# Placing the graph steps of the next groups inside the LSTM of the last layer

## The chip, the cores and the metric

The kernel runs on one core of a Trainium2 chip. The metric is the device time of one execution in microseconds (us), here the median of several runs. Five engines work side by side, each through its own queue of instructions: TensorE (PE), VectorE (DVE), ScalarE (ACT), GpSimd (POOL), and SyncE (SP), which in this kernel issues the DMAs.

## The reference

The program is four graph layers on `x` of shape 128 x 64 x 256 (128 graphs of 64 nodes with 256 features), each added to its input and normalised. Only the last layer matters here. It makes two graph convolutions and then, for each step length p = 1, 2, 3, 4 in turn, runs an LSTM over windows of p nodes and writes the last hidden state over the last node of each window; the next p reads what the one before wrote.

```python
h = jax.nn.relu(jnp.einsum('ts,bsh->bth', adj, x @ Wg0 + bg0))
h = jax.nn.relu(jnp.einsum('ts,bsh->bth', adj, h @ Wg1 + bg1))
for p in range(1, MAX_SKIP + 1):
    nw = Tv // p
    wins = h[:, :nw * p, :].reshape(Bv * nw, p, Hd)
    last = _lstm_last(Wih[p - 1], Whh[p - 1], bih[p - 1], bhh[p - 1], wins)
    idx = jnp.arange(nw) * p + (p - 1)
    h = h.at[:, idx, :].set(last.reshape(Bv, nw, Hd))
...
x = _layernorm(x + _L3_gnn_ref(x, adj, ...), axis=-1)
```

All data are fp32.

## The kernel before, in words

The last layer works on 8 groups of 16 graphs, `g` = 0 to 7. For each group there are three kinds of work.

**The convolutions**, `gcn(g, half, bank, name)`, once for each half of a group. It is a generator of 8 steps, n = 0 to 7. Steps 0 and 1 are the blocks: each loads 256 KB of the layer's residual (`x2r`, L875), applies the batch normalisation of layer 2 with two ACT instructions (L879, in place on the resident tile `A`), turns the data through DRAM (`turned`: a DVE transpose L848, one DMA to the scratch tensor `way` L851, four DMAs back L853), adds on DVE (L884), layer-normalises (DVE statistics, POOL L83 and L97) and stores two pieces to DRAM (L895). Group 0 alone turns by PE (L889) in place of the DMAs. Step 2 multiplies by the neighbour matrix (PE L866, copies L902 on DVE and L903 on ACT), steps 3 and 4 by the first weight (PE L909, DVE L911, ACT L913), steps 5 and 6 by the second (PE L921, DVE L924), step 7 by the neighbours again (PE L866, DVE L932 and ACT L933), which fills the group's tile `H`.

**The LSTM**, `lstm(g)`, is a generator of 22 units, u = 0 to 21. A unit is one of the two 128-row halves `j` of the hidden state, for one time step: units 0 to 3 are p = 1 (two stretches of windows), 4 to 7 p = 2, 8 to 13 p = 3, 14 to 21 p = 4. In a unit PE adds the input part of the gates (L970) and, from the second time step on, the hidden part (L976) in PSUM banks `l` (5 of them), ACT takes the gates out (L982), DVE and POOL form the cell (L985 to L989), ACT takes its tanh (L990). With the second unit of a time step DVE writes the hidden state: `hid` (L999) for the next time step, or back into `H` (L999) at the end of p = 1, 2, 3, or `hd` (L997) at the end of p = 4. So every odd unit ends with a hand-over that a later matmul waits for.

**The output**, `final(g, s)`, for four residues s of the node: a copy on POOL (L1011), the same `turned`, an add (L1024), a layer normalisation and two stores (L1033). It is traced behind units 14, 16 and 18 of its own group, and behind unit 0 of the next group for s = 3.

The order on each engine is not written by hand. A planner takes the instructions as they are traced, gives the earlier traced the higher priority, and on each engine issues what it expects to be ready at that moment. An instruction that is traced late can therefore stand early in an engine's queue, if its inputs are expected early. While group g is in the LSTM, the steps of group g + 1 are traced between its units: `steps_of` gives their order (both halves' blocks, then the rest of half 0, then the rest of half 1), and the loop at the end hands out 16 steps evenly over the first 19 units. All buffers involved rotate: `st` has 5 (two for `turned`, one for an output or a step's result), `g` 3 PSUM banks, `x2r` 4, `way` 4, `hT` 2.

Of the kernel before, what the change touches and what calls it, by code (L numbers as in the profile page):

```python
# [34 lines left out]
SKIP = 4  # L35
# [6 lines left out]
def kernel(ctx: ExitStack, tc: tile.TileContext, i, out):  # L42
    nc = tc.nc
# [41 lines left out]
    def layernorm(dst, src, n, engine):  # L85

        st = small.tile([P, n, 6], F32, name="ln_st", bufs=6)
        mv = small.tile([P, n, 2], F32, name="ln_mv", bufs=6)
        both = small.tile([P, 2, n], F32, name="ln_rs", bufs=6)
        rs, ng = both[:, 0, :], both[:, 1, :]  # L90
        for r in range(n):
            nc.vector.bn_stats(st[:, r, :], src[:, r, :])
            nc.vector.bn_aggr(mv[:, r, :], st[:, r, :])
        rsqrt(rs, mv[:, :, 1], n)
        nc.vector.tensor_scalar_mul(ng, mv[:, :, 0], -1.0)  # L95
        for r in range(n):
            engine.tensor_scalar(dst[:, r, :], src[:, r, :], ng[:, r:r + 1], rs[:, r:r + 1],  # L97
                                 op0=OP.add, op1=OP.mult)
# [725 lines left out]
    NG = NB // GB  # L824
    assert GB * N == 2 * QT

    def gbank(shape):
        return ps.tile([P] + shape, F32, name="g", bufs=3)
# [15 lines left out]
    def turned(src):  # L844


        t = work.tile([P, 4, 4, 32], F32, name="st", bufs=ST)
        nc.vector.transpose(t, src.rearrange("p n (j t) -> p j n t", t=32))  # L848
        o = work.tile([P, 4, 4, 32], F32, name="st", bufs=ST)
        way = dram.tile([P, 4, P], F32, name="way", bufs=4)  # L850
        nc.sync.dma_start(way, t.rearrange("p j n f -> p j (n f)"))  # L851
        for j in range(4):
            nc.sync.dma_start(o[j * 32:(j + 1) * 32].rearrange("t i n f -> t i (n f)"),  # L853
                              way[:, j, :].rearrange("(i t) x -> t i x", t=32))
        return o.rearrange("p i (c m) f -> p c m i f", m=KD)
# [80 lines left out]
    GCN_STEPS = 8  # L936
# [67 lines left out]
    def final(g, s, pieces=1):  # L1004

        if s == SKIP - 1:
            h = lasts.pop(g)
        else:
            h = work.tile([P, 2, KD, P], F32, name="hd", bufs=3)
            for c in range(2):  # L1010
                nc.gpsimd.tensor_copy(h[:, c].rearrange("p k (w b) -> p k w b", b=GB),  # L1011
                                      Hs[g].rearrange("p k (c w s) b -> p c k w s b", c=2, s=SKIP)[:, c, :, :, s, :])

        rows = [v[g * GB:(g + 1) * GB].rearrange("b (c w s) d -> s c w b d", c=2, s=SKIP)[s]
                for v in (x3_dram, out_view)]
        xr = work.tile([P, 2, D], F32, name="x3r")
        for c in range(2):
            nc.sync.dma_start(xr[:, c, :], rows[0][c])
        o = work.tile([P, 2, D], F32, name="st", bufs=ST)
        for cs in ([(0, 1)] if pieces == 1 else [(0,), (1,)]):  # L1020
            r = slice(cs[0], cs[-1] + 1)
            if pieces == 1:
                xv = xr.rearrange("p c (m i f) -> p c m i f", m=KD, f=32)
                nc.vector.tensor_add(xv, turned(h.rearrange("p c m t -> p (c m) t")), xv)  # L1024
            else:
                ht = gbank([2, D])
                for c in cs:
                    for k in range(KD):
                        nc.tensor.transpose(ht[:, c, k * P:(k + 1) * P], h[:, c, k], ident)
                nc.vector.tensor_add(xr[:, r], ht[:, r], xr[:, r])  # L1030
            layernorm(o[:, r], xr[:, r], len(cs), nc.gpsimd)
            for c in cs:
                nc.sync.dma_start(rows[1][c], o[:, c, :])  # L1033

    def steps_of(g):

        if g:
            parts = [gcn(g, half, gbank, "hT") for half in range(2)]
            order = [0, 0, 1, 1] + [0] * (GCN_STEPS - 2) + [1] * (GCN_STEPS - 2)
        else:  # L1040
            parts = [gcn(g, 0, gbank, "hT"), gcn(g, 1, lbank, "hid")]
            order = [0, 0, 1, 1] + [0, 1] * (GCN_STEPS - 2)
        for half in order:
            next(parts[half])
            yield

    for _ in steps_of(0):
        pass
    n_units = sum(-(-(N // p) // (QT // GB)) * p * KD for p in range(1, SKIP + 1))
    first4 = n_units - SKIP * KD  # L1050
    for g in range(NG):

        side = steps_of(g + 1) if g + 1 < NG else iter(())
        n_side, done = 2 * GCN_STEPS, 0
        for u, _ in enumerate(lstm(g)):
            if u == 0 and g:
                final(g - 1, SKIP - 1)
            s, odd = divmod(u - first4, 2)
            if not odd and 0 <= s < SKIP - 1:
                final(g, s)  # L1060
            while done < min(n_side, (u + 1) * n_side / (n_units - 2)):
                next(side, None)
                done += 1
    final(NG - 1, SKIP - 1, pieces=2)


# [38 lines left out]
```

## Time and profile before

| what | value |
|---|---|
| runs | 2173.53, 2174.7, 2179.28 us; median 2174.7 |
| profiled execution | 2175.27 us, its span 2173.4 us |
| the LSTM's part of the span | about 832 to 2173 us: seven groups of some 168.6 us, and the last one of some 161 |
| LSTM matmuls on PE, whole kernel | L970 789.2 us, L976 436.2 us |
| a unit of p = 4 with both parts, on PE | 3.45 us for 16 records of L970, 3.45 us for 16 of L976 |
| granted TensorE clock, mean | 0.986 |
| DMA share of 16 engines, queue 1 | 17.7% |

A time such as "789.2" is busy time: what the records of that line last in sum. "Idle before ... <-" in a row says for how long the engine stood still before that instruction and what ended it. PE's records count every 128-row fp32 multiplication twice.

### The profile page before, as it was taken

To read this page: it belongs to the slowest core of one execution; us is meant where nothing else is said; L and a number is where in the kernel's file an instruction comes from. 1 tells how busy PE (TensorE), PEld (TensorE's weight loads), DVE (VectorE), ACT (ScalarE), POOL (GpSimd) and SP (SyncE) were. 2 spreads that over 40 slices of the span, in tenths; PEclk is the share of its full clock that TensorE was granted. 3 is DMA by queue.
4 is the path that set the end of the run, shared out by engine and by line. 5 is a ranking of instruction groups with operands and counts; after the bars stand their busy time and mean duration, and the time that the engine had idled before them with its cause. 6 is when DMAs were issued, how large, how long until landed. Compare 5 with 4: busy or idle time off the path is not lost.

```text
span 2173.4 us, 29437 instructions
## 1 busy us (share of the span) xinstructions
PE 2083.1 (96%) x11463; PEld 1340.8 (62%) x11463; DVE 863.1 (40%) x2054; ACT 946.2 (44%) x1825; POOL 414.7 (19%) x569
## 2 busy tenths in 40 slices
PE   6999999998999979999999999999999999999997
PEld 4667677775454444576576577477468468468466
DVE  7355555454543444134233323323323423423223
ACT  3766666765338153234233334333333333333332
POOL 1123332433210012011111111111211211202012
PEclk9999999999999979999999999999999999999999
DMA  4023213232222022012112101201201201201001
GB/s 124 20 42 52 50 44 50 52 52 42 42 86 59 0 87 79 0 44 67 46 31 66 60 29 54 73 14 55 88 10 58 89 4 60 73 1 59 20 5 54
DMA packets 169275, 105.54 MB, mean 49 GB/s; under 512 B 86832, under 2 KB 152368, under 8 KB 168880
## 3 DMA queue, kind: packets, MB, share of 16 engines
q1 hardware_dynamic: 167280, 101.70, 17.7%
q8 instruction: 90, 1.47, 0.3%
q0 software_dynamic: 1024, 1.05, 0.2%
q10 hardware_dynamic: 832, 0.92, 0.1%
q14 instruction: 49, 0.40, 0.1%
HBM read 59.59 MB, written 44.04 MB: 48 GB/s over the span
## 4 chain that ended last, share of the span: by engine, by line
PE 80%; ACT 6%; DVE 6%; DMA 3%; issue 2%; POOL 1%; SPq 1%; DVEq 0%; POOLq 0%; ACTq 0%
PE l L970 31%; PE l L976 19%; PE pz L707 5%; PE pz L772 4%; PE e L311 3%; PE g L909 2%; PE g L921 2%; PE m L283 2%; PE m L218 2%; PE m L286 2%; PE g L866 1%; DMA way<-st 1%; PE z L320 1%; PE m L401 1%; PE m L197 1%
## 5 line engine op out<-in xcount | busy, mean ns | idle before, releaser
L970 PE MATMUL l<-H,wih 128*128 128x256 f32 (+2 forms) x2496 | 789.2, 471 | 9.4 <-ACT gate_g L990 3.9
L970 PEld LDWEIGHTS l<-H,wih 128*128 128x128 f32 x2496 | 469.9, 190 | 302.3 <-issue 189.2
L976 PE MATMUL l<-hid,whh 128*128 128x256 f32 (+2 forms) x1536 | 436.2, 437 | 2.1 <-DVE hid L999 2.1
L976 PEld LDWEIGHTS l<-hid,whh 128*128 128x128 f32 x1536 | 291.8, 190 | 130.9 <-issue 61.2
L982 ACT ACTIVATE gate_i<-l,bias 128x256 f32<-128x256 f32 (+2 forms) x176 | 100.1, 569 | 517.8 <-PE l L976 445.9
L985 DVE TENSOR_TENSOR gate_i<-gate_i,gate_g 128x256 f32<-128x256 f32 (+2 forms) x96 | 48.5, 506 | 432.7 <-ACT gate_g L982 432.6
L986 POOL TENSOR_TENSOR cell<-gate_f,cell 128x256 f32<-128x256 f32 (+2 forms) x96 | 84.4, 880 | 670.6 <-ACT gate_f L982 663.4
L83 POOL TENSOR_TENSOR ln_rs<-ln_rs,mhalf 128x2 f32<-128x2 f32 (+2 forms) x97 | 79.1, 815 | 689.5 <-DVE ln_rs L95 689.1
L322 ACT ACTIVATE u<-z 128x1024 f32<-128x1024 f32 x128 | 130.4, 1026 | 57.4 <-PE z L320 56.6
L982 ACT ACTIVATE gate_g<-l,bias 128x256 f32<-128x256 f32 (+2 forms) x176 | 100.3, 570 | 98.3 <-PE l L970 50.1
L990 ACT ACTIVATE gate_g<-cell 128x256 f32<-128x256 f32 (+2 forms) x176 | 90.0, 511 | 88.7 <-DVE cell L989 45.7
L982 ACT ACTIVATE gate_o<-l,bias 128x256 f32<-128x256 f32 (+2 forms) x176 | 99.4, 565 | 61.9 <-PE l L976 54.0
L707 PE MATMUL pz<-A,w 128*128 128x512 f32 x256 | 113.1, 595 | 0.0
L989 DVE TENSOR_TENSOR cell<-gate_i,gate_g 128x512 f32<-128x512 f32 (+2 forms) x80 | 50.0, 624 | 138.1 <-ACT gate_g L982 137.9
L294 DVE TENSOR_TENSOR qs<-m,qs 64x256 fp32r<-64x256 f32 x128 | 54.0, 422 | 124.4 <-ACT qs L293 122.7
L320 PE MATMUL z<-gath_r,qs 128*128 128x512 f32 x256 | 99.4, 476 | 0.6 <-ACT u L322 0.4
L707 PEld LDWEIGHTS pz<-A,w 128*128 128x128 f32 x256 | 47.9, 190 | 55.3 <-issue 53.6
L283 PE MATMUL m<-wq,tT 128*128 128x260 f32 x256 | 72.4, 406 | 8.1 <-ACT yT L391 5.4
L982 ACT ACTIVATE gate_f<-l,bias 128x256 f32<-128x256 f32 (+2 forms) x96 | 51.1, 532 | 59.8 <-PE l L976 59.8
L999 DVE TENSOR_TENSOR hid<-gate_o,gate_g 128x256 f32<-128x256 f32 (+2 forms) x96 | 48.6, 507 | 67.8 <-ACT gate_g L990 39.8
L999 DVE TENSOR_TENSOR H<-gate_o,gate_g 128x512 f32<-128x512 f32 (+1 forms) x64 | 40.9, 639 | 80.7 <-PE l L970 68.5
L286 PE MATMUL m<-wv,tT 128*128 128x256 f32 x256 | 67.3, 386 | 0.6 <-ACT v L296 0.5
(241 smaller groups left out, 2515.2 us busy)
## 6 DMA issues: line engine op xcount, KB each, us to landing
way<-st SPq DMA_DIRECT2D x59, 256.0 KB
st<-way SPq DMA_DIRECT2D x236, 64.0 KB
xin<-in_x SPq DMA_DIRECT2D x16, 512.0 KB
ld<-table SPq DMA_DIRECT2D x16, 512.0 KB
x_dram<-y SPq DMA_DIRECT2D x16, 512.0 KB
x2r<-x_dram SPq DMA_DIRECT2D x32, 256.0 KB
x_dram<-A SPq DMA_DIRECT2D x64, 128.0 KB
x3r<-x_dram SPq DMA_DIRECT2D x64, 128.0 KB
```

Source lines behind the costliest of these rows:

```text
L283: nc.tensor.matmul(pq, xT[:, k, c * P:(c + 1) * P], wq[:, k, :], start=k == 0, stop=k == KD - 1)
L286: nc.tensor.matmul(pv[:, c % 2, :], xT[:, k, c * P:(c + 1) * P], wv[:, k, :], start=k == 0, stop=k == KD - 1)
L320: nc.tensor.matmul(z[:, k, :], L1[q]["qs"][c][:, s, k * P:(k + 1) * P], gath_r, start=True, stop=True)
L322: nc.scalar.activation(u, z, AF.Relu)
L707: nc.tensor.matmul(p_, w1[:, k, m * P:(m + 1) * P], A[:, q, k * QT:(k + 1) * QT], start=k == 0, stop=k == KD - 1)
L772: nc.tensor.matmul(p_, w2[:, k, m * P:(m + 1) * P], hidden(q, k), start=k == 0, stop=k == M1 - 1)
L970: nc.tensor.matmul(gates[n], wih[p][:, k, mw * P:(mw + 1) * P], Hw[:, k, :, s, :], start=k == 0, stop=not s and k == KD - 1)
L976: nc.tensor.matmul(gates[n], whh[p][:, k, m * P:(m + 1) * P], hid[:, k], start=False, stop=k == KD - 1)
L982: nc.scalar.activation(act[n], gates[n], AF.Tanh if n == "g" else AF.Sigmoid, bias=bias[:, p - 1, m:m + 1])
L986: nc.gpsimd.tensor_tensor(cell[:, j], act["f"], cell[:, j], OP.mult)
L990: nc.scalar.activation(act["g"], cell[:, j], AF.Tanh)
L999: nc.vector.tensor_mul(Hw[:, jj, :, s, :] if over else new[:, jj], o, t)
```

## The change

The even hand-out goes. A table `AT` names, for each half and each step, the unit behind which the step is traced, counted from the start of the group before it; a negative number reaches back into the group before that (-5 is unit 17, -3 is unit 19). For group 1, where there is no such group, half 1 starts with units 0, 1, 3, 5, 5. Half 0's blocks come behind units 5 and 6, half 1's behind units 17 and 19 of the period before. Steps 3 and 4, and steps 5 and 6, stand in pairs, half 1's behind units 3 and 7 (the ends of p = 1 and p = 2), half 0's behind 9 and 13 (13 is the end of p = 3). Where one unit has several steps, those with n of 5 or more are traced first.

What is traced behind a unit is now inside `tc.issue_after(...)`: each ACT instruction of these steps stands, in ACT's queue, behind the last ACT instruction traced of that unit (its L990). This fixes an order of issue and adds no semaphore. It holds for ACT alone. The start for group 0 has the same order as before. `gcn`, `lstm` and `final` are unchanged.

```diff
-    def steps_of(g):
-
-        if g:
-            parts = [gcn(g, half, gbank, "hT") for half in range(2)]
-            order = [0, 0, 1, 1] + [0] * (GCN_STEPS - 2) + [1] * (GCN_STEPS - 2)
-        else:
-            parts = [gcn(g, 0, gbank, "hT"), gcn(g, 1, lbank, "hid")]
-            order = [0, 0, 1, 1] + [0, 1] * (GCN_STEPS - 2)
-        for half in order:
-            next(parts[half])
-            yield
-
-    for _ in steps_of(0):
-        pass
+    parts = [gcn(0, 0, gbank, "hT"), gcn(0, 1, lbank, "hid")]
+    for half in [0, 0, 1, 1] + [0, 1] * (GCN_STEPS - 2):
+        next(parts[half])
+
     n_units = sum(-(-(N // p) // (QT // GB)) * p * KD for p in range(1, SKIP + 1))
     first4 = n_units - SKIP * KD
+    AT = [[5, 6, 7, 9, 9, 13, 13, 15], [-5, -3, 1, 3, 3, 7, 7, 11]]
+    side = {}
+    for g in range(1, NG):
+        for half in range(2):
+            part = gcn(g, half, gbank, "hT")
+            at = AT[half] if g > 1 or not half else [0, 1, 3, 5, 5] + AT[half][5:]
+            for n, u in enumerate(at):
+                side.setdefault((g - 1) * n_units + u, []).append((n >= 5, part))
     for g in range(NG):
-
-        side = steps_of(g + 1) if g + 1 < NG else iter(())
-        n_side, done = 2 * GCN_STEPS, 0
         for u, _ in enumerate(lstm(g)):
-            if u == 0 and g:
-                final(g - 1, SKIP - 1)
-            s, odd = divmod(u - first4, 2)
-            if not odd and 0 <= s < SKIP - 1:
-                final(g, s)
-            while done < min(n_side, (u + 1) * n_side / (n_units - 2)):
-                next(side, None)
-                done += 1
+            traced = nc.cur_bb.bb.instructions
+            with tc.issue_after([t for t in traced[-200:] if t.engine == mybir.EngineType.Activation][-1]):
+                if u == 0 and g:
+                    final(g - 1, SKIP - 1)
+                s, odd = divmod(u - first4, 2)
+                if not odd and 0 <= s < SKIP - 1:
+                    final(g, s)
+                for _, part in sorted(side.pop(g * n_units + u, []), key=lambda t: not t[0]):
+                    next(part)
     final(NG - 1, SKIP - 1, pieces=2)
```

## The prediction

> **What bounds the kernel now.** I began with the page's first part. Then I cut the span into the eight LSTM periods with the table of stretches, since the change touches nothing else by name.
>
> ```profile
> PE 2083.1 (96%) x11463; PEld 1340.8 (62%) x11463; DVE 863.1 (40%) x2054; ACT 946.2 (44%) x1825; POOL 414.7 (19%) x569
> ```
> ```profile
> 1169.19:1338.02 168.83, 167.49 (x809) 108.48 (x809) 57.51 (x133) 59.67 (x108) 27.92 (x42) 1.00 0.16 51
> 1338.02:1506.39 168.37, 167.50 (x810) 108.49 (x809) 57.60 (x133) 59.67 (x108) 27.89 (x42) 1.00 0.16 51
> 2012.02:2173.40 161.38, 149.39 (x509) 95.56 (x507) 43.06 (x101) 54.73 (x102) 22.95 (x34) 0.99 0.09 27
> ```
>
> After each stretch's length stands PE's busy time. A period is PE's own work (167.5 us) and about one microsecond of standing still. The change moves PE work and removes none, so inside the periods only those idle pieces can be won. The list of waits says what they are for the whole LSTM (total, times, longest):
>
> ```profile
> PE l L970 <- ACT gate_g L990: 3.9, 8, 0.6
> PE l L970 <- DVE H L999: 3.5, 5, 0.9
> PE l L976 <- DVE hid L999: 2.1, 1, 2.1
> ```
>
> PE's and DVE's timelines show where the first two lie: the end of p = 1, where p = 2 reads what DVE writes back to `H`.
>
> ```profile
> 1359.10 2.81 PE L970 MATMUL l<-H,wih 128*128 128x512 f32 x6 [0.48 <-ACT gate_g L990]
> 1362.31 7.99 PE L970 MATMUL l<-H,wih 128*128 128x512 f32 x18 [0.39 <-DVE H L999]
> ```
> ```profile
> 1360.96 0.69 DVE L884 TENSOR_TENSOR x2r<-st,x2r 128x512 f32<-128x512 f32 x1 [2.00 <-DMA st<-way]
> 1361.56 0.69 DVE L999 TENSOR_TENSOR H<-gate_o,gate_g 128x512 f32<-128x512 f32 x1
> ```
>
> The write of `H` stands in DVE's queue behind a block's add L884, which waits for its DMA. Only then did I read the start of the layer, since what the planner may issue early is issued early. ACT, then PE, then DVE:
>
> ```profile
> 779.89 31.55 ACT L879 ACTIVATE A<-A,sh,sc 128x256 f32<-128x256 f32 x64 [64.62 <-DVE sh L692]
> 811.34 0.57 ACT L903 ACTIVATE hT<-g 128x512 f32<-128x512 f32 x1
> ```
> ```profile
> 806.78 1.24 PE L866 MATMUL l<-bdT,A 64*64 64x64 f32 x32 [0.62 <-POOL A L97]
> 811.96 3.78 PE L909 MATMUL g<-hT,wg 128*128 128x512 f32 x4 [3.94 <-ACT hT L903]
> ```
> ```profile
> 830.70 0.69 DVE L848 STREAM_TRANSPOSE st<-A 128x512 f32<-128x512 f32 x1
> 831.29 1.00 DVE L932 TENSOR_SCALAR H<-l 128x512 f32<-128x512 f32 x1
> ```
>
> All 64 normalisations L879, of all eight groups, run in one piece before anything else; only 8 are group 0's. Group 0's copy L903 stands behind them, and PE waits 3.94 us for it.
>
> **What the Trainium skill says.** "PSUM — Partial Sum Buffer", section "Engine vs sequencer instructions": the queues of ACT, DVE and POOL are strictly first in, first out, and matmuls start and finish in program order. The trace agrees: L999 behind L884 (2.00 us), L903 behind 64 L879. "DMA: Bandwidth & Descriptors", section "Anatomy of one DMA": a DMA has about 2 us of fixed cost, mostly the receipt of the write. It says so for another issuing path than SP's, but SP stands 108.4 us over 59 round trips between `way` and `st`, 1.8 us each, which agrees. "TensorE: Matmul & The Clock Gate", Part 1: after idle time the clock is granted at half rate. Between 801 and 808 us the table of stretches shows 0.50, and the L909 of 811.96 lasts 3.78 us where later ones last 1.88. No page prices the planner's order.
>
> **The change, part by part.**
>
> *Order on ACT at the start.* 56 of the 64 L879 (31.55 / 64 = 0.49 us each) get behind L990s of the LSTM. ACT is then free when PE has finished group 0's neighbours: first half by 804.3, second by 808.0. L903 is ready before PE is free; PE goes on at 808.0 instead of 811.96. Gain 3.9 us. The rest of the start, up to 829.5, is PE in one piece and moves up whole; the half-rate stretch comes along (it follows the idle time before it), so I take nothing for the clock; 0 to 2 us are possible. The two L848 of group 1 in DVE's queue before L932 at 831.29 also go, since they now wait for an L879 behind unit 0; L932 could end about 0.6 us earlier, and PE's first L970 (832.39) follows its end. I take 0.6. Sum 4.5 us; the bounds are 0.5 (another thing, such as POOL's L97 chain until 807.3, holds L903 anyway) and 6.5.
>
> *End of p = 1 (unit 3).* Blocks leave p = 1, so no L884 stands before L999 there. From group 2 on, half 1's steps 3 and 4 lie right behind unit 3: 2 x 1.72 = 3.43 us of PE work whose inputs are ready, while L999 needs some 0.3 us for the first half of `H` and less than 2 us for the second. It covers the whole wait. The two waits sum to 7.4 us; without the last period's 0.48 and the first's 0.57 (where step 2 stands behind unit 3 and depends on fresh DMAs) 6.3 us in six periods. Gain 6.3, bounds 5 and 6.9.
>
> *Ends of p = 2 and 3 (units 7, 13).* No wait there before, because a step of 1.7 us lay there; now two do. Zero. Unit 7's four `g` banks against three exist: the fourth waits for L924, which runs beside step 6's 1.7 us. Zero.
>
> *L879 inside the periods.* Eight a period, 3.9 us of ACT, which is busy 60 of 168. Behind a waiting pair stands only the next unit's gate_i, due 3.45 + 0.86 us after the unit's end at p = 4; L990 ends some 1.1 us after it, two L879 take 1.0. Covered by 2 us. No wait is added for another engine.
>
> *Blocks behind units 5, 6 and 17, 19.* Each brings 8 DMAs (1 load, 1 out, 4 back, 2 stores, some 4 us of SP issue), a DVE add that waits for them, and POOL's L83 and L97, 1.8 to 2.7 us. From L848 to L1024 or L884 takes about 6 to 10 us (for example 1353.30 to 1360.96). Behind odd units the add thus falls into the middle of the following even unit and the next odd one's beginning, not at a hand-over: at p = 2 a unit lasts 13.7 us, at p = 4 6.9, a pair 13.8. Half 0's second block is needed by step 2 behind unit 7, about 3 us later than it is done. I take zero for the blocks alone.
>
> *p = 4 loses its cover.* Before, steps 5, 6 and 7 of half 1 (1.7, 1.7, 1.1 us) stood behind units 16, 17 and 18. Now nothing stands behind 16 to 21. What they covered (DVE, POOL, PE):
>
> ```profile
> 1978.79 0.69 DVE L1024 TENSOR_TENSOR x3r<-st,x3r 128x512 f32<-128x512 f32 x1 [4.44 <-DMA st<-way]
> ...
> 1983.38 0.42 DVE L987 TENSOR_TENSOR cell<-cell,gate_i 128x256 f32<-128x256 f32 x1 [1.69 <-POOL cell L986]
> ```
> ```profile
> 1981.57 1.09 POOL L97 TENSOR_SCALAR st<-x3r,ln_rs 128x256 f32<-128x256 f32 x2
> 1982.62 0.72 POOL L986 TENSOR_TENSOR cell<-gate_f,cell 128x256 f32<-128x256 f32 x1
> ```
> ```profile
> 1981.21 1.89 PE L921 MATMUL g<-wg,hT 128*128 128x256 f32 x8
> 1982.94 3.62 PE L970 MATMUL l<-H,wih 128*128 128x256 f32 x16
> ```
>
> The output's chain reaches unit 17's hand-over late: `hid` is written by 1984.76, and PE, thanks to L921, asks for it at 1986.39, 1.6 us later. Without L921 and with unit 17 ending 0.6 us earlier (side work between units 13 and 17: 3.45 + 1.1 against 3.43 + 1.73) it asks at 1984.1: 0.7 to 0.9 us short. The last period has no side work and shows both outcomes: no wait at its unit 17, since the planner put L1024 behind `hid` there, and 2.13 us at unit 19:
>
> ```profile
> 2149.38 0.69 DVE L1024 TENSOR_TENSOR x3r<-st,x3r 128x512 f32<-128x512 f32 x1 [6.40 <-DMA st<-way]
> ```
>
> I take half of 0.9, 0.45 us in each of seven periods: 3.2 us lost. Bounds: 0, and 0.9 at unit 17 and 2.1 at unit 19 in each of six to seven, about 20 us.
>
> *Last period and tail*: no side work, unchanged.
>
> Sum: -4.5 - 6.3 + 3.2 = -7.6 us. The profiled execution took 2175.27 us (span 2173.4 and 1.9 around it), so 2167.7; from the median 2174.7 of the runs it is 2167.1, which I forecast.
>
> **The rivals.**
> 1. *Nothing is given back*: the planner sees the LSTM's instructions as due first and puts L1024 behind `hid`, as in the last period's unit 17. 2174.7 - 10.8 = 2163.9. Against it: DVE blocked 4.1 to 4.5 us at that place in every earlier period.
> 2. *p = 4 gives most back*: 0.9 at unit 17 in seven periods and some 0.2 at unit 19, in sum 7.6: 2171.5, no change that can be told. The same result comes if the start's 3.9 us were held by something else.
> 3. *Slower*: with the extra block, SP's one queue (three outputs of 4.8 us and two blocks of 4: 22 us of issue in some 50) delays each round trip, and DVE stands before a `way` DMA at both hand-overs, units 17 and 19. At 2 x 2.1 us in six periods 25 us, less 10.8: 2189. It decides from 1.8 us a period on, and is slower by what can be measured from 2.9. For it: the wait of 6.40 us with no extra block at all. Against it: blocks are half a pair away from the outputs.
>
> **How the numbers follow.** A measurement of this kernel tells about 0.3% (6.5 us) from no change. Chances: forecast 0.38 (its own range 2164 to 2171, on both sides of the bound of 2168.2: 0.27 faster, 0.11 same), rival 1 0.18 (0.17 faster, 0.01 same), rival 2 0.28 (0.26 same, 0.01 on each side), rival 3 0.16 slower. Together faster 0.45, same 0.38, slower 0.17. The range 2162 to 2181 holds all but the far part of rival 3 and a little below rival 1.
>
> **What would show it.** Right: 8 L879 in one piece at 780 us and pairs after it; the wait of L909 for L903 gone and the first L970 near 828; no PE wait at the end of p = 1 from the second period on. Wrong: L970 still at 832, or L976 waiting for `hid` in each period for more than 0.5 us. More than 1.8 us of such waits a period would turn the sign.

## The result, and the profile after

| | runs | median | ratio to before, 95% interval |
|---|---|---|---|
| before, on the same chip | 4 | 2176.23 us (2173.53 to 2179.28) | |
| after | 4 | 2179.89 us (2173.85 to 2181.13) | 1.0011 [0.9987, 1.0035] |

The change makes no difference that can be told. The time of 2167.1 us that was forecast lies 12.8 us below the median; the measured one is near the upper end of the range, 2162 to 2181. So the gain that was worked out is missing, and the question is whether it never came or was given back.

The page of after, its first part and one group of its fifth (busy time, mean ns of one | idle time before it and what ended most of it):

```profile
PE 2084.7 (96%) x11463; PEld 1344.5 (62%) x11463; DVE 870.7 (40%) x2054; ACT 947.0 (43%) x1825; POOL 417.4 (19%) x569
...
L976 PE MATMUL l<-hid,whh 128*128 128x256 f32 (+2 forms) x1536 | 448.1, 445 | 16.3 <-DVE hid L999 16.2
```

PE's busy time is up by 1.6 us, and that of L976 alone from 436.2 to 448.1 us for the same 1536 records. PE also stands 16.2 us for `hid`, before 2.1. The list of waits, over the LSTM (total, times, longest), confirms this and shows what has gone:

```profile
PE l L976 <- DVE hid L999: 16.2, 8, 3.4
...
PE l L970 <- ACT gate_g L990: 0.5, 1, 0.5
```

Of the waits at the end of p = 1 (3.9 and 3.5 us) only the last period's 0.48 is left. To place gains and losses I cut both spans at two points: the first L879, where the code that differs begins, and the first L970, where the LSTM begins.

| profiled execution | first L879 at | start: to the first L970 | LSTM: from there to the end | span |
|---|---|---|---|---|
| before | 779.89 | 52.50 | 1341.0 | 2173.4 |
| after | 775.16 | 46.53 | 1357.3 | 2179.0 |

The first column is the earlier layers, which are the same code: over 13 profiled executions it goes from 775.2 to 782.1. The two other columns are the change: the start gained 6.0 us, the LSTM lost 16.3.

**The start.** ACT's timeline of after, then PE's:

```profile
775.16 2.07 ACT L879 ACTIVATE A<-A,sh,sc 128x256 f32<-128x256 f32 x4 [64.63 <-DVE sh L692]
790.01 2.08 ACT L879 ACTIVATE A<-A,sh,sc 128x256 f32<-128x256 f32 x4 [12.78 <-DVE sh L692]
799.52 0.60 ACT L903 ACTIVATE hT<-g 128x512 f32<-128x512 f32 x1 [7.44 <-PE g L866]
```
```profile
803.07 3.29 PE L909 MATMUL g<-hT,wg 128*128 128x512 f32 x4
...
821.69 8.85 PE L970 MATMUL l<-H,wih 128*128 128x512 f32 x20 [1.26 <-ACT H L933]
```

Only group 0's 8 normalisations are left in front. L903 now waits for PE, not PE for L903. L909 begins 27.91 us after the first L879, before 32.07: 4.2 us. From L909 to the first L970 it takes 18.62 us, before 20.43: 1.8 us more, 0.5 of it in the shorter first L909, which still runs at the lower clock.

**The end of p = 1**, PE's timeline of after in the first period:

```profile
1006.28 10.57 PE L970 MATMUL l<-H,wih 128*128 128x512 f32 x24
1016.68 3.60 PE L909 MATMUL g<-hT,wg 128*128 128x512 f32 x8
1020.12 2.31 PE L970 MATMUL l<-H,wih 128*128 128x512 f32 x5
```

The pair of step 3 and 4 (L909) lies between unit 3 and p = 2, and the L970 after it shows no wait.

**Where it went.** The same timeline over the whole LSTM, the records that waited for `hid` (one more, at 1307.18, waited 0.18):

```profile
983.08 4.97 PE L976 MATMUL l<-hid,whh 128*128 128x256 f32 x14 [2.72 <-DVE hid L999]
...
1153.69 3.29 PE L976 MATMUL l<-hid,whh 128*128 128x256 f32 x14 [1.81 <-DVE hid L999]
...
1323.72 4.98 PE L976 MATMUL l<-hid,whh 128*128 128x256 f32 x14 [2.46 <-DVE hid L999]
...
1495.95 6.28 PE L976 MATMUL l<-hid,whh 128*128 128x256 f32 x14 [3.42 <-DVE hid L999]
...
1668.24 4.98 PE L976 MATMUL l<-hid,whh 128*128 128x256 f32 x14 [2.17 <-DVE hid L999]
...
1839.32 4.97 PE L976 MATMUL l<-hid,whh 128*128 128x256 f32 x14 [2.26 <-DVE hid L999]
...
2158.67 3.29 PE L976 MATMUL l<-hid,whh 128*128 128x256 f32 x14 [1.14 <-DVE hid L999]
```

One wait in each of the first six periods, always at unit 19's hand-over, 14.8 us in sum; 0.18 us once at unit 17; the last period's wait fell from 2.13 to 1.14. The second number of each line is the other half of the loss: the 14 records last 3.29 us after a short wait and 4.97 to 6.28 after most of the long ones. Five of them are above 3.29, by 1.68, 1.69, 2.99, 1.69 and 1.68, or 9.7 us in sum. The table of stretches says why (length, PE's busy time, granted clock, DMA share, GB/s):

```profile
983.00:988.00 5.00, 4.92 (x15) 0.66 0.22 64
1153.70:1157.00 3.30, 3.30 (x15) 1.00 0.31 93
...
1496.00:1502.00 6.00, 6.00 (x14) 0.50 0.23 63
```

After a wait of 2.72 us the clock is at 0.66 of full speed on the mean over 5 us, after 3.42 at 0.50 over 6, after 1.81 at 1.00. If the clock is either full or half, 0.66 over 5 us is 3.4 us at half rate, and that costs the 1.7 us. The account of the LSTM: 14.8 + 0.2 + 9.7 lost at p = 4, 1.0 gained in the last period, 6.9 gained at the end of p = 1. That is 16.8 us lost, where 16.3 were measured.

**Why `hid` is late at unit 19.** DVE, POOL and SP's queue in the second period of after, around the block behind unit 17. Its transposed data leave DVE at 1138.04 and come back for L884 at 1147.47:

```profile
1133.27 1.12 DVE L1024 TENSOR_TENSOR x3r<-st,x3r 128x512 f32<-128x512 f32 x1 [4.38 <-DMA st<-way]
...
1138.04 0.71 DVE L848 STREAM_TRANSPOSE st<-A 128x512 f32<-128x512 f32 x1 [0.56 <-ACT A L879]
...
1147.47 0.69 DVE L884 TENSOR_TENSOR x2r<-st,x2r 128x512 f32<-128x512 f32 x1 [4.78 <-DMA st<-way]
...
1149.35 0.42 DVE L985 TENSOR_TENSOR gate_i<-gate_i,gate_g 128x256 f32<-128x256 f32 x1
1152.24 0.42 DVE L987 TENSOR_TENSOR cell<-cell,gate_i 128x256 f32<-128x256 f32 x1 [2.47 <-POOL cell L986]
1153.21 0.42 DVE L999 TENSOR_TENSOR hid<-gate_o,gate_g 128x256 f32<-128x256 f32 x1 [0.54 <-ACT gate_g L990]
```
```profile
1149.46 0.87 POOL L83 TENSOR_TENSOR ln_rs<-ln_rs,mhalf 128x2 f32<-128x2 f32 x1 [8.71 <-DVE ln_rs L95]
1150.43 1.09 POOL L97 TENSOR_SCALAR A<-x2r,ln_rs 128x256 f32<-128x256 f32 x2
1151.49 0.72 POOL L986 TENSOR_TENSOR cell<-gate_f,cell 128x256 f32<-128x256 f32 x1
```
```profile
1137.22 1.35 SPq L1033 DMA_DIRECT2D out<-st  x2
1138.67 1.27 SPq L1018 DMA_DIRECT2D x3r<-x_dram  x2
1140.05 0.43 SPq L851 DMA_DIRECT2D way<-st  x1
1144.05 1.73 SPq L853 DMA_DIRECT2D st<-way  x4
```

DVE stands 4.78 us before the block's add L884. Unit 19's L985 is queued behind it, then its L986 on POOL behind the block's L83 and L97, then L987, L990 and L999. On SP an output's two stores and the next output's two loads stand ahead of the block's `way`. The block therefore needs 9.4 us from L848 to L884, and ends at a hand-over. It also starts late: the output's L1024 at 1133.27, which waited 4.38 us for its own DMA, holds up unit 17's chain, and the block's L879 stand behind unit 17's L990.

The other periods fit. Over the six, this trip takes 10.36, 9.43, 9.82, 11.05, 9.81 and 9.89 us. In five of them PE's wait is the trip less 7.62 to 7.64 us, in the third, whose unit 17 was itself late, less 7.36. A trip of under some 7.4 us would by this estimate cost nothing here.

### The profile page after: what moved, and what is told of

Same layout as the page of the kernel before. It is cut to its first block, busy times and chain, and to the rows that moved or that the text cites. A ratio compares the mean times of both kernels' runs of the same rounds, so it can differ in the third digit from the quotient of the medians.

```text
span 2179.0 us, 29406 instructions
## 1 busy us (share of the span) xinstructions
PE 2084.7 (96%) x11463; PEld 1344.5 (62%) x11463; DVE 870.7 (40%) x2054; ACT 947.0 (43%) x1825; POOL 417.4 (19%) x569
## 4 chain that ended last, share of the span: by engine, by line
PE 75%; DVE 8%; ACT 6%; DMA 5%; issue 2%; POOL 2%; SPq 2%; DVEq 0%; POOLq 0%; ACTq 0%
PE l L970 30%; PE l L976 15%; PE pz L772 5%; PE pz L707 5%; DMA way<-st 3%; PE e L311 3%; PE g L909 2%; PE m L283 2%; PE g L921 2%; PE m L218 2%; DMA st<-way 2%; PE m L286 2%; PE m L401 1%; PE z L320 1%; PE g L866 1%
## 5 line engine op out<-in xcount | busy, mean ns | idle before, releaser
L970 PE MATMUL l<-H,wih 128*128 128x256 f32 (+2 forms) x2496 | 787.5, 470 | 1.9 <-ACT H L933 1.3
L970 PEld LDWEIGHTS l<-H,wih 128*128 128x128 f32 x2496 | 471.6, 190 | 286.4 <-issue 186.1
L976 PE MATMUL l<-hid,whh 128*128 128x256 f32 (+2 forms) x1536 | 448.1, 445 | 16.3 <-DVE hid L999 16.2
L976 PEld LDWEIGHTS l<-hid,whh 128*128 128x128 f32 x1536 | 297.7, 194 | 150.7 <-issue 61.0
L986 POOL TENSOR_TENSOR cell<-gate_f,cell 128x256 f32<-128x256 f32 (+2 forms) x96 | 84.0, 875 | 795.1 <-ACT gate_f L982 795.1
L83 POOL TENSOR_TENSOR ln_rs<-ln_rs,mhalf 128x2 f32<-128x2 f32 (+2 forms) x97 | 80.9, 834 | 569.8 <-DVE ln_rs L95 569.3
L985 DVE TENSOR_TENSOR gate_i<-gate_i,gate_g 128x256 f32<-128x256 f32 (+2 forms) x96 | 48.5, 505 | 317.3 <-ACT gate_g L982 317.3
L990 ACT ACTIVATE gate_g<-cell 128x256 f32<-128x256 f32 (+2 forms) x176 | 90.0, 511 | 127.8 <-DVE cell L987 60.4
L999 DVE TENSOR_TENSOR hid<-gate_o,gate_g 128x256 f32<-128x256 f32 (+2 forms) x96 | 48.3, 503 | 75.3 <-ACT gate_g L990 39.5
L999 DVE TENSOR_TENSOR H<-gate_o,gate_g 128x512 f32<-128x512 f32 (+1 forms) x64 | 41.0, 641 | 71.1 <-PE l L970 54.1
L879 ACT ACTIVATE A<-A,sh,sc 128x256 f32<-128x256 f32 x64 | 34.3, 586 | 77.4 <-DVE sh L692 77.4
```

The lines of the kernel that those rows point to most:

```text
L83: nc.gpsimd.tensor_tensor(dst, dst, mhalf[:, :n], OP.pow)
L970: nc.tensor.matmul(gates[n], wih[p][:, k, mw * P:(mw + 1) * P], Hw[:, k, :, s, :], start=k == 0, stop=not s and k == KD - 1)
L976: nc.tensor.matmul(gates[n], whh[p][:, k, m * P:(m + 1) * P], hid[:, k], start=False, stop=k == KD - 1)
L986: nc.gpsimd.tensor_tensor(cell[:, j], act["f"], cell[:, j], OP.mult)
L990: nc.scalar.activation(act["g"], cell[:, j], AF.Tanh)
L999: nc.vector.tensor_mul(Hw[:, jj, :, s, :] if over else new[:, jj], o, t)
```

## The experiments

A "wait at unit 19" is PE's L976 for the `hid` that unit 19 hands over; "start" and "LSTM" are the two columns of the table above.

**e1: the blocks leave p = 4.**

```diff
-    AT = [[5, 6, 7, 9, 9, 13, 13, 15], [-5, -3, 1, 3, 3, 7, 7, 11]]
+    AT = [[5, 6, 7, 9, 9, 13, 13, 15], [-13, -11, 1, 3, 3, 7, 7, 11]]
```

> The changed kernel with one edit: half 1's blocks behind units 9 and 11 of the period before (p = 3) in place of 17 and 19 (p = 4); nothing else moves. Theory A (the block behind unit 17 brings a DVE add that waits for its DMA, and a normalisation on POOL, in front of unit 19's cell): the six PE waits of 1.8 to 3.4 us at unit 19 and the slow matmuls after them go, the LSTM part falls from 1357 us to about 1333, the time to about 2158 (ratio to before 0.992). Theory B (the waits come from the output's own chain, because PE steps no longer stand in p = 4; the blocks only happen to be near): the waits stay, 2178 to 2182. Theory C (the order on ACT inside the periods delays the LSTM): the waits stay too.

Measured: 2161.26 us, ratio 0.9937 [0.992, 0.9954]; start 46.88, LSTM 1333.2. All waits at unit 19 but the last period's (1.44) are gone, with nothing put in as cover. Behind units 9 and 11 of p = 3 the round trip of a block is short. DVE and SP's queue of e1:

```profile
904.17 0.70 DVE L848 STREAM_TRANSPOSE st<-A 128x512 f32<-128x512 f32 x1
...
910.26 0.69 DVE L884 TENSOR_TENSOR x2r<-st,x2r 128x512 f32<-128x512 f32 x1 [4.29 <-DMA st<-way]
```
```profile
904.90 0.32 SPq L851 DMA_DIRECT2D way<-st  x1
906.89 1.74 SPq L853 DMA_DIRECT2D st<-way  x4
```

DVE still stands 4.29 us, but between hand-overs, and the trip takes 6.1 us in place of 9.4. Over all periods these trips take 6.0 to 6.2 us.

**e2: cover put back at p = 4.** Half 0's last three steps go behind units 19, 19 and 20; the blocks stay.

```diff
-    AT = [[5, 6, 7, 9, 9, 13, 13, 15], [-5, -3, 1, 3, 3, 7, 7, 11]]
+    AT = [[5, 6, 7, 9, 9, 19, 19, 20], [-5, -3, 1, 3, 3, 7, 7, 11]]
```

> The changed kernel with half 0's steps 5 and 6 behind unit 19 and step 7 behind unit 20, in place of 13, 13 and 15; the blocks stay at 17 and 19. 3.4 us of PE work then lies on the hand-over of unit 19. Theories A and B both: the waits for hid at unit 19 shrink to below 0.5 us each and no slow matmuls follow, some 20 us less. What the pair did behind unit 13 is lost: if it covered the write of H at the end of p = 3, PE now waits there, up to 1.9 us in each of seven periods, so about 2172 in all; if unit 13 needs no cover, 2160. Theory C: little changes.

Measured: 2177.91 us, 1.0009 [1.0, 1.0018]; LSTM 1348.4. The time missed what was expected. The covered waits did go (only the last period's, 2.21, is left), and unit 13 without its pair shows none either. But the steps that were moved wait themselves, since DVE stands before an output's L1024 ahead of their L924 (DVE, then PE, of e2):

```profile
988.84 0.69 DVE L1024 TENSOR_TENSOR x3r<-st,x3r 128x512 f32<-128x512 f32 x1 [3.44 <-DMA st<-way]
...
990.72 1.28 DVE L924 TENSOR_TENSOR st<-g,bg 128x512 f32<-128x512 f32 x2
```
```profile
991.46 1.29 PE L866 MATMUL g<-bdT,st 64*64 64x64 f32 x64 [1.34 <-DVE st L924]
```

This wait comes in five periods (7.3 us in all). The second block's L884 then stands 6.81 us at 1002.76, and p = 1 begins with a wait for `gate_i` in five (3.2 us). One of the five waits of L866, of 2.03 us, also has slow records behind it (below, on the hardware). Cover hides a wait at one place; a DVE that stands before DMAs is late at the next.

**e3: the order on ACT is taken away.**

```diff
-            with tc.issue_after([t for t in traced[-200:] if t.engine == mybir.EngineType.Activation][-1]):
+            with ExitStack():
```

> The changed kernel without the order on ACT (the table of units stays). All 64 L879 run at the start again: from the first L879 to the first L970 52 us in place of 46.5, 6 us lost. Theory A: the block's chain in p = 4 starts 1 to 2 us earlier, because it no longer stands behind unit 17's L990 and the two L879, so the waits at unit 19 shrink by a third to a half, 8 to 12 us won; in sum about 2176. Theory B: waits as in the changed kernel, in sum 2186. Theory C: the waits vanish, 2162.

Measured: 2204.25 us, 1.0129 [1.0113, 1.0146]; start 52.87, LSTM 1370.6. None of the numbers expected came near. The start is that of before, so the gain there comes from this order alone. The six waits at unit 19 are gone; two of 1.14 and 0.67 us stand at unit 17, and the last period keeps its 1.21 at unit 19. In their place there are six of 3.1 to 5.4 us at the end of p = 1, slow records behind five of them. DVE and PE of e3:

```profile
1020.19 0.70 DVE L848 STREAM_TRANSPOSE st<-A 128x512 f32<-128x512 f32 x1
...
1030.58 0.69 DVE L884 TENSOR_TENSOR x2r<-st,x2r 128x512 f32<-128x512 f32 x1 [5.40 <-DMA st<-way]
...
1031.65 0.67 DVE L999 TENSOR_TENSOR H<-gate_o,gate_g 128x512 f32<-128x512 f32 x1
```
```profile
1032.38 7.94 PE L970 MATMUL l<-H,wih 128*128 128x512 f32 x12 [4.79 <-DVE H L999]
```

With all L879 done at the start, a block's transpose has no input to wait for. The planner takes two blocks up at the end of p = 1, before the units that the table names (by their place those of units 5 and 6; the trace does not name them), and L884 stands there before the write of `H`. This is the wait of before, larger. So the order on ACT, by holding L879 back, also keeps the blocks in their place on DVE.

**e4: the kernel before with that order alone.** The even hand-out stays, inside `tc.issue_after(...)`.

```diff
+            traced = nc.cur_bb.bb.instructions
+            with tc.issue_after([t for t in traced[-200:] if t.engine == mybir.EngineType.Activation][-1]):
...
-            while done < min(n_side, (u + 1) * n_side / (n_units - 2)):
+                while done < min(n_side, (u + 1) * n_side / (n_units - 2)):
```

> The kernel before with its own even hand-out, and only the order on ACT added. Start: only 8 L879 before the LSTM, 46.5 us in place of 52.5 from the first L879 to the first L970. Theories A and B: the LSTM part stays at 1341 within 3 us, so about 2169 (ratio 0.997). Theory C: the LSTM part grows by 10 us or more, 2178 or above.

Measured: 2168.62 us, 0.9967 [0.9955, 0.998]; start 46.22, LSTM 1342.9. The start is gained, the waits at the end of p = 1 stay (3.6 for `H` and 3.4 for `gate_g`), and only the last period's wait at unit 19 moved, from 2.13 to 2.79. The part of the change that pays at the start is thus worth 6.3 us by itself.

**e5: one block alone leaves p = 4** (-5 becomes -13, -3 stays).

```diff
-    AT = [[5, 6, 7, 9, 9, 13, 13, 15], [-5, -3, 1, 3, 3, 7, 7, 11]]
+    AT = [[5, 6, 7, 9, 9, 13, 13, 15], [-13, -3, 1, 3, 3, 7, 7, 11]]
```

> The changed kernel with only the first of half 1's two blocks moved, from unit 17 to unit 9 (p = 3); the second stays behind unit 19. Theory A in its narrow form (the block behind unit 17 is the one that lands on unit 19's hand-over; the one behind unit 19 lands on unit 21's, which no matmul of the LSTM waits for): all six waits at unit 19 go, LSTM part 1333 to 1336 us as with both moved, about 2163. Rival (two blocks in p = 4 load the DMA queue and POOL, each worth about half): waits of 1 us or so stay, LSTM part about 1345, 2173.

Measured: 2160.76 us, 0.9932 [0.9915, 0.9948]; LSTM 1334.6. At unit 19 only the last period's wait is left, 1.30. One of 1.17 stands at unit 17, behind an output's L1024 that waited 5.85 us for its DMA. It is the block behind unit 17 that costs; that behind unit 19, by itself, costs nothing that can be told (e1, without it, 1333.2). The block behind unit 17 by itself was not run.

**e6: the last step of the block's normalisation (L97) on DVE in place of POOL**, to price L97 ahead of L986. L83 stays on POOL.

```diff
-            layernorm(x3, x, 2, nc.gpsimd)
+            layernorm(x3, x, 2, nc.vector if g else nc.gpsimd)
```

> The changed kernel, both blocks in p = 4, with the last step of the blocks' layer normalisation (L97) on DVE in place of POOL for groups 1 to 7. Theory A with POOL's part: of the wait at unit 19 about 1.1 us is L97 in front of L986, so the waits fall from 1.8 to 3.4 us to 0.7 to 2.3 us, most of the slow matmuls after them go, LSTM part about 1345 in place of 1357. Rival (the DMA wait of L884 on DVE is all of it): the two instructions on DVE make it no better, 1355 to 1360.

Measured: 2175.05 us, 0.9995 [0.9984, 1.0006]; LSTM 1345.4. The six waits sum to 10.2 us in place of 14.8. Only the first, 2.48, is followed by slow records (4.98). So 4.7 us less of waiting saved 8.0 us of slow matmuls. The rest of the waits is DVE standing before the DMA:

```profile
1142.38 0.71 DVE L848 STREAM_TRANSPOSE st<-A 128x512 f32<-128x512 f32 x1 [0.56 <-ACT A L879]
...
1152.19 0.69 DVE L884 TENSOR_TENSOR x2r<-st,x2r 128x512 f32<-128x512 f32 x1 [5.16 <-DMA st<-way]
...
1157.43 0.42 DVE L999 TENSOR_TENSOR hid<-gate_o,gate_g 128x256 f32<-128x256 f32 x1 [0.54 <-ACT gate_g L990]
```

From L884 to L999 it is 5.2 us here, 5.7 in after; the trip before it is as long as there (9.8 and 9.4).

**e7 and e8: are the pairs needed?** Both have e1's blocks. e7 takes the pairs apart, e8 leaves nothing but step 2 near unit 3.

```diff
-    AT = [[5, 6, 7, 9, 9, 13, 13, 15], [-5, -3, 1, 3, 3, 7, 7, 11]]
+    AT = [[5, 6, 7, 8, 9, 12, 13, 15], [-13, -11, 1, 2, 3, 6, 7, 11]]
```

> Blocks at units 9 and 11 as in e1_blocks_p3, and the three pairs parted: one step behind units 3, 7, 9 and 13, the other one unit earlier (2, 6, 8, 12). If one step of 1.7 us is enough at an end of p = 1, 2, 3, the LSTM part is 1333 us as in e1_blocks_p3 within 2; if the pairs matter, PE waits for H at one of these ends, 0.5 us or more in each of six periods, 1336 or more.

```diff
-    AT = [[5, 6, 7, 9, 9, 13, 13, 15], [-5, -3, 1, 3, 3, 7, 7, 11]]
+    AT = [[5, 6, 7, 9, 9, 13, 13, 15], [-13, -11, 1, 5, 5, 7, 7, 11]]
```

> As e1_blocks_p3, with half 1's steps 3 and 4 behind unit 5 in place of unit 3: no PE step at the end of p = 1, and no block's add in DVE's queue there either. If the add L884 alone made the waits of before, they stay away: LSTM part 1333. If PE work was needed as cover, the wait for the first half of H comes back, 0.5 us in six periods, and the one for the second half (0.4 to 0.9) does not: 1336. Both back: 1340.

Measured: e7 2161.49 us, 0.9941 [0.9924, 0.9958], LSTM 1332.8; e8 2161.69 us, 0.994 [0.9923, 0.9956], LSTM 1335.0. Neither has a wait at the end of p = 1 but the last period's. PE's timeline of e8 shows how the gap closes without a step there:

```profile
1014.47 1.02 PE L909 MATMUL g<-hT,wg 128*128 128x512 f32 x2
1015.32 5.18 PE L970 MATMUL l<-H,wih 128*128 128x512 f32 x11
```

In each of the six periods the planner pulled one multiplication of step 3, traced behind unit 5, into the gap, since step 2 was done early. What closes it is PE work that is ready, and a DVE without an L884 before L999. The last period, in before as in e8, has neither a step nor an L884 there; it keeps 0.48 us for `gate_g` and none for `H`. So L884 made the wait for `H`, and the 0.48 is what PE work has to cover. A pair is more than it takes.

**e9: the outputs are moved, the blocks stay where the change put them.** Outputs 1 and 2 are traced behind units 20 and 21 in place of 16 and 18.

```diff
-                s, odd = divmod(u - first4, 2)
-                if not odd and 0 <= s < SKIP - 1:
+                s = {14: 0, 20: 1, 21: 2}.get(u)
+                if s is not None:
```

> The changed kernel, blocks at 17 and 19, with the outputs for s = 1 and 2 traced behind units 20 and 21 in place of 16 and 18. Sharper form of theory A: the block behind unit 17 alone would be harmless (6.1 us from L848 to L884, as at unit 9); it lands on unit 19's hand-over because the output's two stores and two loads stand before it in SP's queue and slow its way through DRAM (9.4 us). Then the waits at unit 19 go, LSTM part 1335 to 1340, about 2165. Rival (the block itself is enough): waits stay near 2 us, LSTM part 1350 or more. If the planner pulls the outputs forward all the same, this run doesn't tell them apart.

Measured: 2160.65 us, 0.9936 [0.9917, 0.9956]; LSTM 1332.3. No wait for `hid` in any period, the last one included. DVE and SP's queue of e9 at the place that was shown of after:

```profile
1136.44 0.71 DVE L848 STREAM_TRANSPOSE st<-A 128x512 f32<-128x512 f32 x1 [0.56 <-ACT A L879]
...
1143.17 0.69 DVE L884 TENSOR_TENSOR x2r<-st,x2r 128x512 f32<-128x512 f32 x1 [0.38 <-DMA st<-way]
...
1149.28 0.42 DVE L999 TENSOR_TENSOR hid<-gate_o,gate_g 128x256 f32<-128x256 f32 x1 [0.54 <-ACT gate_g L990]
```
```profile
1137.18 0.34 SPq L851 DMA_DIRECT2D way<-st  x1
1139.86 1.73 SPq L853 DMA_DIRECT2D st<-way  x4
```

The same block behind the same unit takes 6.7 us here, and 6.3 to 6.7 over the six periods. DVE stands 0.38 us for it, behind unit 18's work, and unit 19's chain begins on time. The block alone is harmless; the block together with the outputs is not.

The two traces also say in which ways the outputs did it, since PE is at the same place of its work in both within 0.1 us. L884 begins 4.3 us earlier in e9: 1.6 us because L848 begins earlier (no L1024 ahead of unit 17's chain), 1.3 because `way` is issued 0.7 us after L848 begins and not 2.0 (no stores and loads ahead of it on SP), 1.3 because the way out takes 2.7 us and not 4.0, issue to issue; the way back differs by 0.1.

**e10: the blocks behind even units** (-4 and -2, units 18 and 20).

```diff
-    AT = [[5, 6, 7, 9, 9, 13, 13, 15], [-5, -3, 1, 3, 3, 7, 7, 11]]
+    AT = [[5, 6, 7, 9, 9, 13, 13, 15], [-4, -2, 1, 3, 3, 7, 7, 11]]
```

> The changed kernel with half 1's blocks behind units 18 and 20 in place of 17 and 19, one unit later. If the planner expects the DMA back too early and puts L884 before unit 19's hidden state, DVE stands there until some 4 us after the unit's end: waits of 3 to 6 us in six periods, LSTM part 1370 or more. If it puts L884 behind the hidden state, no matmul waits: 1335. Theories B and C: no change, 1357.

Measured: 2166.7 us, 0.9966 [0.9956, 0.9975]; LSTM 1343.2, between what was expected. At unit 19 none of the six waits is left, as the planner puts L884 behind `hid` there (L999 at 1152.58, L884 at 1158.30); one of 0.47 us stands at unit 17. The block behind unit 20 is late instead for step 2 of its own half, in three periods (PE of e10):

```profile
1344.15 1.00 PE L866 MATMUL g<-bdT,A 64*64 64x64 f32 x32 [1.31 <-POOL A L97]
```

The last period's wait grew to 3.52 us, with slow records behind it.

**e11: both remedies**, e1's blocks and e9's outputs.

```diff
-    AT = [[5, 6, 7, 9, 9, 13, 13, 15], [-5, -3, 1, 3, 3, 7, 7, 11]]
+    AT = [[5, 6, 7, 9, 9, 13, 13, 15], [-13, -11, 1, 3, 3, 7, 7, 11]]
...
-                s, odd = divmod(u - first4, 2)
-                if not odd and 0 <= s < SKIP - 1:
+                s = {14: 0, 20: 1, 21: 2}.get(u)
+                if s is not None:
```

> Both remedies at once: half 1's blocks behind units 9 and 11, and the outputs for s = 1 and 2 behind units 20 and 21. If PE is the bound once the waits are gone, nothing adds up: LSTM part 1332 us as with each alone, about 2160 (ratio 0.993). If each alone left something, 1328 or less.

Measured: 2159.84 us, 0.9933 [0.9919, 0.9946]. The two gains do not add: e1, e5, e7, e8 and e9 lie at 2160.65 to 2161.69 us too. In e11 PE's waits from the first L970 on, beyond the 1.2 us at that L970 itself, sum to 2.3 us, and PE is busy for 1318.3 of the LSTM's 1332.7; PE's own work is nearly all that is left. These versions are 0.6 to 0.7% faster than before; after did not run beside them, but its median is higher by 18 us or more.

## Why the prediction was right and wrong

**Order on ACT at the start**: right, its size a little low. 4.5 us were put down, 6.0 measured. e3 loses it and e4 has it alone, so the cause is shown.

**End of p = 1**: right. 6.3 us were put down; in after 6.9 of the 7.4 us of waits are gone. The reason given, pairs as cover, is only half of it: e7 and e8 close the gap with less, and the wait for `H` is gone because L884 is.

**Ends of p = 2 and 3, and L879 inside the periods**, at zero: nothing in after speaks against them; PE has no wait there.

The time lies in the range that was given, but that is luck. The range was laid around a loss of 3.2 us at p = 4, and the loss was 23.7. The two columns of the traces make after 10.3 us slower, more than the 6.3 by which the range reached above before; only the medians, 3.7 us apart, put the time inside. Of the prediction's own signs, those of right came true in the main, and so did one of wrong: L976 waits for `hid` at one hand-over in each of the first six periods, for 1.81 us or more.

**"I take zero for the blocks alone"**: this step failed. The words "alone" and "not at a hand-over" carried it. The durations were right for a trip by itself (6 to 10 us; e1 6.1, e9 6.7), but beside outputs it is at the upper end or past it, 9.4 to 11.1 us, and then L884 stands until unit 19's L985 is overdue. With 1.2 us of statistics, 2.0 us of POOL's L83 and L97 and the chain through L987, L990 and L999 `hid` is 1.8 to 3.4 us late. e5 shows which of the two blocks it is, e9 that it takes the outputs. What the text said against rival 3, "blocks are half a pair away from the outputs", holds by place of tracing and not by SP's queue, where the output traced before is stored and the next one loaded just ahead of `way`. The 1.8 us that SP stands for `way` in before is a mean of 59 waits; the longest of them was already 4.0.

**"p = 4 loses its cover"**, 3.2 us: mis-sized and at the wrong place. Unit 17 cost 0.18 us in one period where 0.45 in seven were counted. The loss came at unit 19, which stood in the bounds with 2.1 us a period and was kept out of the value; it was 2.5 on the mean of six. The lost cover is not the cause, only what would have hidden it: e1, e5 and e9 have no more cover than after.

**The clock behind a wait** had no term at all. The text used the lower clock at the start and did not ask what a new wait of 2 us would do to it. It added 9.7 us to 14.8 us of waiting.

With the measured terms: 6.0 gained at the start and 6.9 at p = 1, against 14.8 + 0.2 + 9.7 lost at p = 4 less 1.0 in the last period. That makes 10.8 us slower by the traces, whose own columns say 16.3 - 6.0 = 10.3. The earlier layers were 4.7 us quicker in the profiled execution of after than in that of before; medians of four runs differ by 3.7 us with an interval from 2.8 quicker to 7.6 slower. So rival 3's mechanism is what happened, at one of its two hand-overs. Its waits alone, 14.8 us, would barely have outweighed the 12.9 us gained; the slow matmuls, which it did not price, make up the rest, and even so the sum is no difference that can be told.

The 3.3 us between the trips of 6.1 in e1 and 9.4 in after can be divided by the lines shown: from L848 to the issue of `way` 0.7 and 2.0 us, from there to the issue of the next `st` 2.0 and 4.0, from there to L884 3.4 in both. Two things stay open. Why the way out takes twice as long behind four other DMAs is not known. The Trainium skill, "DMA: Bandwidth & Descriptors", section "Anatomy of one DMA", has about 2 us of fixed cost, for DMAs that another engine issues; e1's 2.0 us, where SP's queue is otherwise empty, is near that, and after's 4.0 is not. No run issued these DMAs from another engine. And the place at which the clock falls was not sought by itself.

## What to carry to other kernels

When work is moved so that it no longer collides at one hand-over, ask of each of its instructions that waits for a DMA what stands behind it in its engine's queue, and compute the length of the DMA's trip with everything that the issuing queue holds ahead of it there, not from a trip measured elsewhere. A wait on PE can cost more than its own length, when the clock falls behind it; here cutting waits of 2.5 us to 1.7 saved more in clock than in waiting. When several placements reach the same time, as six did here, look at what is left: in e11 PE's waits were 2.3 us of 1332.7, so a further order had little to win.

## What the runs showed of the hardware

The clock can fall after shorter waits than I had thought. The Trainium skill, "TensorE: Matmul & The Clock Gate", Part 1, puts the half rate after at least one idle window of about 3.4 us, and says that the window runs freely. At unit 19's hand-over the 14 records behind a wait lasted 4.97 us or more after 2.17, 2.26, 2.46, 2.72 and 3.42 us in after, 2.48 in e6, 2.79 in e4 and 3.52 in e10. They lasted 3.29 us after 2.13 in before, 2.21 in e2 and every wait up to 1.82. The shortest wait with slow records behind it is in another place, in e2, where 16 records of L970 take 5.41 us in place of 3.72 (after a wait of 1.54 in the period before):

```profile
1331.78 1.29 PE L866 MATMUL g<-bdT,st 64*64 64x64 f32 x64 [2.03 <-DVE st L924]
1333.01 5.41 PE L970 MATMUL l<-H,wih 128*128 128x256 f32 x16
```

So a standstill well below 3.4 us was enough, and between 2.03 and 2.21 both happened. The price hardly grew with the wait: 1.7 us for all of these but the 3.42, which cost 3.0. In e3, in the other place, a wait of 3.08 us left the rate alone (38 records of L970 in 16.57 us, at the usual 0.435 each) where 3.80 us cost 1.7 us. That nearly the same length can go either way agrees with a window that runs freely; the length does not agree, and the measurement decides.

The strict order of DVE's queue, which the Trainium skill states in "PSUM — Partial Sum Buffer", section "Engine vs sequencer instructions", shows in the lines of after, where unit 19's L985 begins only when L884 and its statistics are through. By what stood behind, a stand of DVE before a DMA cost PE nothing (4.29 us in e1, between hand-overs) or microseconds (4.78 us in after, before unit 19's chain: 1.81).
